# Two more node tiles by count matrices in layer 3, layer 4's input loads on ScalarE's queue, and the early products dealt over 48 steps

## The chip, the cores and the metric

The kernel runs on one NeuronCore of a Trainium2 chip. What counts is the device time of one execution in microseconds. The median of three runs of the kernel before is 2790.45 us (2781.69 to 2791.27). TensorE (PE) multiplies, VectorE (DVE) and ScalarE (ACT) work elementwise, GpSimd (POOL) issues the indirect gathers, and SyncE (SP) issues DMAs. Each engine works off its own instructions in order, waits included.

## The reference, cut to what matters

The input is a graph with 6250 nodes and 100000 edges, sorted by destination, and `x` with 256 features a node. Four graph layers follow each other, and the result is added to `x`:

```
h = relu(layernorm(x))
h = sage_mean(h)   # h@W_self + (segment_sum(h[src], dst) / max(deg,1))@W_neigh + b   256 -> 512
h = sage_pool(h)   # hmax = segment_max(relu(h@W_pool + b)[src], dst); h@W_self + hmax@W_neigh + b
h = sage_gcn(h)    # (segment_sum(h[src], dst) + h) / (deg + 1) @ W_neigh + b
h = sage_mean(h)   # like the first, 512 -> 512
out = x + h@W_fc + b_fc    # 256 wide
```

All is f32. The products with weights are pulled ahead of the sums where that is possible, so that each layer mainly sums or maximizes rows of a table over the edges of a node.

## The kernel before, in words

The nodes are `NT` = 49 tiles of 128 (the last has 106 rows), the edges `T` = 782 tiles of 128. There are two ways to sum the neighbours of a node tile:

- **By count matrices.** For a node tile `d` and a source tile `s` a 128 x 128 matrix holds how many edges lead from each node of `s` to each of `d`. These are made once and stored in fp8 in `tab_a`. `dense` (L555 to 579) then takes one product of a count matrix and the rows of `s` after the other (L566 where the rows are f32, L574 where they are split into bf16 or f32r parts, L572 for a tile's own rows) and adds them up in a PSUM bank `pd`.
- **By gathers.** `sums` (L468) takes the edge tiles from node tile `h` on: GpSimd gathers 128 source rows into a slot of `ring` (L492), VectorE makes a one-hot of the destinations (L488), TensorE multiplies both (L513 for bf16 parts, three matmuls each, L510 for f32), and VectorE adds the groups' banks `pg` into the node tile's `acc` (L542, L544). Between two gathers `sums` calls `hub.advance`, which issues a share of the products of the first kind, and moves on generators that finish a node tile.

`HUB` = (H1, H3, H4) = (8, 18, 22) says how many of the first node tiles, which have the most edges, are summed by count matrices in layers 1, 3 and 4.

*Layer 2* (max-pooling, about 732 to 1915 us) runs over 782 steps `at`. In each, GpSimd gathers 128 rows (L1688) and VectorE carries running maxima through them (L1669, called from L1694 to L1705). Beside these steps count matrices are made (up to step `EARLY_AT` = 310), finished node tiles go through `done2` (products `pm_prf`, L1552 to 1558), and their rows for layer 3 go to table `tab_r`. The rows of tiles 8 to 39 (`EARLY`) also go straight into layer 3's sums: `early_products` (L1626) takes them in eight batches and, for each of the first H3 node tiles, issues a load `ae<-tab_a` on SP (L1637), a cast to f32r on ScalarE (L1624), the products (L574, L572) and an add into `acc3[d]` on VectorE (L1306; a tile's first by a copy on ScalarE, L1309). L1732 to 1734 deal this work out: at each step they issue what is left, divided by the number of steps, 32 or less.

*Layer 3* (about 1945 to 2363 us) takes the other source tiles (0 to 7 and 40 to 48) by count matrices for the first 18 node tiles, 43 matmuls a tile (L1878), and all edges of the other node tiles by 314 gathers of `tab_r` (384 KB each). `done3` (L1834) stores halves of the result into `tab_s` (L1865) and a part of the output, `xq` (L1866). Some tiles' halves (`z4_kept`, 12 tiles) stay in SBUF for layer 4.

*Layer 4* (from about 2363 us) loads the others (`z4_late`, 37 tiles, `resident`, L1817, 256 KB a tile), and sums 22 node tiles by count matrices. These stream in chunks: `ac<-tab_a` loads on ScalarE's queue (L1785), casts `af<-ac` on ScalarE two chunks ahead (L1794), 1078 matmuls (L566). The other edges go by 266 gathers of `tab_s`. A node tile ends in `load4` and `finish4`: `load4` loads the rows of `x` and of `xq` into `xr4` and `q4`, of which there are 7 buffers each (L1893, L1895); VectorE adds both (L1909) and twice a scaled half of the sum (L1911), and SP stores the tile from the same buffer `xr4` (L1914). So a load into `xr4` waits until the store of the tile seven before has landed.

A scheduler puts the instructions of each engine into their order when the kernel is built: as a rule it moves a load up to where its buffer comes free, and other work by its own estimates, so the order is not that of the source.

## Time and profile before

| | us |
|---|---|
| median of three runs | 2790.45 |
| lowest, highest | 2781.69, 2791.27 |
| the profiled execution | 2779.08 |
| its span in the trace | 2777.2 |

| stage (us from the start of the span) | length | PE busy | DVE busy | POOL busy |
|---|---|---|---|---|
| layer 1, 0 to 712 | 712 | 621 | 552 | 506 |
| layer 2, 732 to 1915 | 1183 | 914 | 1015 | 801 |
| layer 3, 1945 to 2363 | 418 | 393 | 290 | 313 |
| layer 4, 2363 to 2777 | 414 | 344 | 222 | 254 |

The times of the stages are from one profiled execution, whose granted TensorE clock was 0.915 on the mean. A row of a view of groups or of waits has the engine, the line and the tiles; in a timeline row the start, the duration, the engine, the line, the operation, the output and inputs, the count, and in brackets the idle time before it and what ended it. A matmul's duration in such a row is its whole passage; what it costs the engine is the distance of the starts.

### The profile page before, as it was taken

How to read it: one execution, taken by the hardware profiler on the slowest of the kernel's cores; microseconds unless marked ns; L12 is line 12 of the kernel's file. 1: busy time of each engine (PE TensorE's matmuls, PEld its weight loads, DVE VectorE, ACT ScalarE, POOL GpSimd, SP SyncE). 2: the span in 40 equal slices, each digit the busy share in tenths (PEclk: the TensorE clock that was granted, in tenths of full speed). 3: DMA queues.
4: the chain of work that ended last, by engine and by line, in shares of the span. 5: the costliest groups of instructions: out<-in, count | busy, mean ns of one | idle time of the engine just before them, and what ended most of it. 6: DMA issues, size and time to landing. Idle time of an engine off the chain costs nothing.

```text
span 2777.2 us, 37443 instructions
## 1 busy us (share of the span) xinstructions
PE 2299.6 (83%) x10201; PEld 1418.2 (51%) x10256; DVE 2092.7 (75%) x5568; ACT 1287.6 (46%) x2837; POOL 1877.5 (68%) x2193
## 2 busy tenths in 40 slices
PE   4698999999695566567899999994899999688887
PEld 2356667667443222234555666462444444466776
DVE  8888767766699898796788998786567777355656
ACT  4567767764388888785332333231101010243443
POOL 5477777777567676676656766764777777556664
PEclk8799999999897678688899999997999999799998
DMA  8567777777799999899999999997999999989886
GB/s 269 157 185 204 206 210 215 223 227 219 248 354 323 305 350 325 290 353 346 319 289 317 352 344 307 322 318 234 386 380 392 388 390 358 333 283 294 286 279 201
DMA packets 364121, 818.00 MB, mean 295 GB/s; under 512 B 56271, under 2 KB 151607, under 8 KB 363869
## 3 DMA queue, kind: packets, MB, share of 16 engines
q0 software_dynamic: 145168, 511.30, 56.6%
q1 hardware_dynamic: 157696, 227.59, 22.8%
q10 hardware_dynamic: 61036, 76.62, 8.0%
q8 instruction: 84, 1.38, 0.2%
q14 instruction: 137, 1.11, 0.1%
HBM read 610.63 MB, written 205.46 MB: 294 GB/s over the span
## 4 chain that ended last, share of the span: by engine, by line
PE 42%; DMA 32%; DVE 11%; issue 5%; ACT 4%; POOL 3%; ACTq 0%; SPq 0%; DVEq 0%; POOLq 0%
PE pd L574 13%; PE pg L513 9%; DMA X<-rows,srcIf 8%; DMA ring<-tab_r,srcE 5%; DMA ring<-tab_h,srcT 4%; DVE run L1669 3%; DMA out<-xr 3%; PE pm_hp L1175 3%; PE pm_prf L1558 2%; DMA xr<-in_x 2%; PE pm_w L277 2%; PE pm_hp L1169 2%; DMA rows<-X 2%; DMA zt<-tab_s 2%; PE pb L349 2%
## 5 line engine op out<-in xcount | busy, mean ns | idle before, releaser
L1688 POOL DMA_INDIRECT X<-rows,srcIf x782 | 742.8, 950 | 360.4 <-issue 147.0
L1669 DVE SCALAR_TENSOR_TENSOR run<-run,samef,X 128x512 f32<-128x512 f32 x758 | 571.8, 754 | 49.8 <-DMA X<-rows,srcIf 44.6
L492 POOL DMA_INDIRECT ring<-tab_h,srcT x474 | 455.6, 961 | 149.9 <-issue 52.5
L513 PE MATMUL pg<-ring,hot 128*128 128x256 bf16 (+2 forms) x2344 | 493.1, 317 | 59.2 <-DMA ring<-tab_h,srcT 29.3
L492 POOL DMA_INDIRECT ring<-tab_r,srcE x314 | 314.9, 1003 | 116.2 <-issue 46.3
L544 DVE SCALAR_TENSOR_TENSOR acc<-pg,M,acc 128x256 f32<-128x256 f32 (+2 forms) x629 | 322.5, 539 | 84.4 <-PE pg L513 70.9
L1794 ACT CAST af<-ac 128x768 fp32r<-128x768 fp8e4 (+3 forms) x212 | 171.0, 808 | 435.5 <-DMA ac<-tab_a 175.1
L492 POOL DMA_INDIRECT ring<-tab_s,srcE x266 | 254.2, 955 | 150.9 <-PE pg L510 80.7
L513 PEld LDWEIGHTS <-hot 128*128 128x128 bf16 x2364 | 220.8, 98 | 261.2 <-issue 127.3
L566 PE MATMUL pd<-zt,af 128*128 128x512 f32 x1078 | 309.9, 416 | 30.4 <-ACT af L1794 16.8
L1669 DVE SCALAR_TENSOR_TENSOR X<-X,samef,run 128x512 f32<-128x512 f32 x379 | 281.7, 743 | 40.6 <-DMA X<-rows,srcIf 22.5
L574 PE MATMUL pd<-kept_rows,aw 128*128 128x512 f32 x828 | 259.6, 438 | 11.1 <-ACT aw L1624 5.6
L566 PEld LDWEIGHTS pd<-zt,af 128*128 128x128 f32 x1078 | 215.2, 201 | 86.8 <-ACT af L1794 23.9
L488 DVE TENSOR_SCALAR hot<-iota_bf,keyE 128x128 bf16<-128x128 bf16 (+1 forms) x580 | 147.2, 279 | 97.7 <-PE pg L513 52.0
L1558 PE MATMUL pm_prf<-unf,hTf 128*128 128x512 f32 x384 | 204.3, 659 | 1.9 <-ACT hTf L1548 1.3
L574 PEld LDWEIGHTS pd<-kept_rows,aw 128*128 128x128 f32 x828 | 157.7, 193 | 73.3 <-issue 29.8
L341 ACT ACTIVATE hs<-ht,onef 128x128 bf16<-128x128 bf16 x396 | 153.6, 393 | 87.7 <-PE pb L349 86.6
L574 PE MATMUL pd<-Z,A 128*128 128x256 bf16 (+1 forms) x1176 | 184.1, 273 | 0.9 <-ACT A L354 0.8
L1624 ACT CAST aw<-ae 128x512 fp32r<-128x512 fp8e4 x144 | 89.3, 621 | 161.3 <-PE pd L574 142.8
L375 ACT ACTIVATE ht<-iota_bf,skR 128x128 bf16<-128x128 bf16 x448 | 158.2, 402 | 10.4 <-DMA col<-in_L_gnn_b 7.2
L340 ACT ACTIVATE ht<-iota_bf,sk 128x128 bf16<-128x128 bf16 x396 | 153.2, 398 | 8.3
L488 DVE TENSOR_SCALAR hot<-iota_bf,keyT 128x128 bf16<-128x128 bf16 x474 | 125.4, 274 | 39.5 <-PE pg L513 38.4
(391 smaller groups left out, 4087.9 us busy)
## 6 DMA issues: line engine op xcount, KB each, us to landing
rows<-X SPq DMA_DIRECT2D x385, 256.0 KB
tab_r<-r ACTq DMA_DIRECT2D x48, 384.0 KB
rows<-hpf SPq DMA_DIRECT2D x49, 256.0 KB
th<-tab_t ACTq DMA_DIRECT2D x49, 256.0 KB
X<-rows,srcIf POOLq DMA_INDIRECT x782
tab_a<-A ACTq DMA_DIRECT2D x14, 784.0 KB
ac<-tab_a ACTq DMA_DIRECT2D x110, 96.0 KB
tab_t<-th SPq DMA_DIRECT2D x37, 256.0 KB
```

Source lines behind the costliest of these rows:

```text
L341: nc.scalar.activation(hots[0], t, AF.Relu, bias=one, scale=-1.0)
L375: nc.scalar.activation(held["ht"][:, i, :], iota_b, AF.Abs, bias=sk[:, r : r + 1])
L488: nc.vector.tensor_scalar(hot[j], iota_b, keyT[:, j - jb : j - jb + 1], None, op0=ALU.is_equal)
L492: nc.gpsimd.indirect_dma_start(out=ring[:, j % deep, :].bitcast(F32) if wide else ring[:, j % deep, :], out_offset=None, in_=table, in_off ...
L513: mm = nc.tensor.matmul(pg[:, : F + c], hot[j], X[:, part * F : (part + 1) * F + c], start=(k == 0 and part == 2), stop=(k == n - 1 and pa ...
L544: nc.vector.scalar_tensor_tensor(acc[d], half, m, acc[d], op0=ALU.mult, op1=ALU.add)
L566: nc.tensor.matmul(hold[0], a, z, start=(s == ss[0]), stop=(s == ss[-1]))
L574: nc.tensor.matmul(hold[0][:, : F + c], a, z[:, part * F : (part + 1) * F + c], start=(first and s != own), stop=(s == ss[-1] and part == ...
L1558: nc.tensor.matmul(pm, hT[:, c, :], un[:, c, :], start=False, stop=(c == KH - 1))
L1669: nc.vector.scalar_tensor_tensor(put, held, st, row, op0=ALU.mult, op1=ALU.max)
L1688: nc.gpsimd.indirect_dma_start(out=X[:, k, :], out_offset=None, in_=tab_p, in_offset=bass.IndirectOffsetOnAxis(ap=srcI[:, t : t + 1], axis=0),
L1794: nc.scalar.copy(wide[i][:, :n, :], got[i][:, :n, :])
```

## The change

Three things change. H3 goes from 18 to 20: node tiles 18 and 19 are summed in layer 3 by count matrices. (These exist already, since layer 4 uses 22 tiles.) The early products are dealt over 48 steps where it was 32. In layer 4 the loads of `x` and `xq` are issued on ScalarE's queue, with ten buffers each, and the tiles that stay in SBUF are now 10 (33 to 42), with 39 loaded back.

```diff
@@ -28,7 +28,7 @@
 BLOCKS = (52, 100, 220, 180, 130, 100)
 Z_SIGMA = 5.0
 WIN, WIN2 = 8, 4
-HUB = (8, 18, 22)
+HUB = (8, 20, 22)
 EARLY = (8, 40)
 MADE_AT = 64
 FIRST_AT = 112
@@ -1731,7 +1731,7 @@
                         copies.pop(0)()
                     if at > EARLY_AT + 10:
                         early.advance(early.done + math.ceil(
-                            early.left() / max(1, min(32, T - 24 - at))))
+                            early.left() / max(1, min(48, T - 24 - at))))
                     if b == 0 and s0 == 0 and k == 0:
                         for _ in finding:
                             pass
@@ -1824,8 +1824,8 @@
         psm = on.enter_context(tc.tile_pool(name="psm3", bufs=2, space=PSUM))
         zk = on.enter_context(tc.tile_pool(name="fz4", bufs=1, side="right"))
         Z4 = {}
-        z4_kept = ((31, 37), (37, 43))
-        z4_late = ((0, 7), (7, 14), (14, 20), (20, 26), (26, 31), (43, NT))
+        z4_kept = ((33, 38), (38, 43))
+        z4_late = ((0, 7), (7, 14), (14, 20), (20, 27), (27, 33), (43, NT))
         for s0, s1 in z4_kept:
             zt = zk.tile([P, s1 - s0, 2 * FO], F32R, name=f"zt{s0}", bufs=1)
             Z4.update({s: zt[:, s - s0, :] for s in range(s0, s1)})
@@ -1889,10 +1889,10 @@
 
             def load4(d):
                 n = P if d < NFULL else NREM
-                xr = wk.tile([P, FI], F32, name="xr4", bufs=7)
-                nc.sync.dma_start(xr[:n, :], x[d * P : d * P + n, :])
-                q = wk.tile([P, FO], F32, name="q4", bufs=7)
-                nc.sync.dma_start(q[:n, :], xq[d * P : d * P + n, :])
+                xr = wk.tile([P, FI], F32, name="xr4", bufs=10)
+                nc.scalar.dma_start(xr[:n, :], x[d * P : d * P + n, :])
+                q = wk.tile([P, FO], F32, name="q4", bufs=10)
+                nc.scalar.dma_start(q[:n, :], xq[d * P : d * P + n, :])
                 loaded4[d] = n, xr, q
 
             def done4(d, acc):
```

On the engines' orders this gives: L574 has 3316 matmuls, before 3102, L572 40, before 36, and L513 2292, before 2364; 290 gathers of `tab_r`, before 314; 140 adds at L1306, before 126; 160 loads and casts `ae`, `aw`, before 144. The matmuls at L566 and L510 and the gathers of `tab_s` stay as many.

SyncE in the middle of layer 4, before. `xr4_...` are allocations of the residual buffers, numbers grow in program order; `in_x` is the input, `xq_70` the part of the output from layer 3:

```order
L1914 DMA out_0<-xr4_25672 128x256
L1893 DMA xr4_26104<-in_x 128x256
L1914 DMA out_0<-xr4_25557 128x256
L1893 DMA xr4_26171<-in_x 128x256
L1895 DMA q4_26653<-xq_70 128x256
L1895 DMA q4_26666<-xq_70 128x256
L1914 DMA out_0<-xr4_25720 128x256
L1893 DMA xr4_26267<-in_x 128x256
```

The same engine after, at the same stores of layer 4:

```order
L1914 DMA out_0<-xr4_25846 128x256
L1914 DMA out_0<-xr4_25716 128x256
L1914 DMA out_0<-xr4_25884 128x256
L1914 DMA out_0<-xr4_26016 128x256
L1914 DMA out_0<-xr4_25993 128x256
```

Only the stores are left. Before, the load into `xr4_26104` waited for the store from `xr4_25672` ahead of it, since it takes its buffer, and the store from `xr4_25557` stood behind that load.

ScalarE after, at the same place. `af` is a cast chunk of count matrices, `ac` a loaded one:

```order
L1794 CAST af_25877<-ac_25751 128x768
L1785 DMA ac_25955<-tab_a_69 128x384
L1794 CAST af_25912<-ac_25770 128x896
L1893 DMA xr4_26504<-in_x 128x256
L1785 DMA ac_25974<-tab_a_69 128x384
L1794 CAST af_25931<-ac_25792 128x768
L1785 DMA ac_25988<-tab_a_69 128x320
L1893 DMA xr4_26554<-in_x 128x256
L1794 CAST af_25953<-ac_25811 128x768
L1895 DMA q4_27226<-xq_70 128x256
```

The load into `xr4_26504` waits for the landing of the store from `xr4_25846`, that into `xr4_26554` for the one from `xr4_25716`; the casts behind them wait with them. Before, this queue had only casts and `ac` loads here.

VectorE in layer 4, before: from the last use of a buffer (`xr4_26005`) to the add on the tile that is loaded into it next (`xr4_26488`). `acc` are sums of node tiles, `hot` one-hots:

```order
L1911 SCALAR_TENSOR_TENSOR xr4_26005<-pd_25846,rmeanf_128,xr4_26005 128x256 x2
L544 SCALAR_TENSOR_TENSOR acc_25832<-pg_25998,M_125,acc_25832 128x256
L488 TENSOR_SCALAR hot_26095<-iota_bf_109,keyE_10816 128x128
L544 SCALAR_TENSOR_TENSOR acc_25832<-pg_25998,M_125,acc_25832 128x256
L544 SCALAR_TENSOR_TENSOR acc_25995<-pg_25998,M_125,acc_25995 128x256
L488 TENSOR_SCALAR hot_26115<-iota_bf_109,keyE_10816 128x128
L544 SCALAR_TENSOR_TENSOR acc_25995<-pg_25998,M_125,acc_25995 128x256
L488 TENSOR_SCALAR hot_26127<-iota_bf_109,keyE_10816 128x128
L1909 TENSOR_TENSOR xr4_26386<-xr4_26386,q4_26388 128x256
L488 TENSOR_SCALAR hot_26139<-iota_bf_109,keyE_10816 128x128
L1909 TENSOR_TENSOR xr4_26488<-xr4_26488,q4_26490 128x256
```

After: from the row behind the last use of `xr4_25683` to the add on the tile that takes its buffer, `xr4_26341`:

```order
L544 SCALAR_TENSOR_TENSOR acc_25443<-pg_25663,M_125,acc_25443 128x256
L488 TENSOR_SCALAR hot_25763<-iota_bf_109,keyE_10816 128x128
L544 SCALAR_TENSOR_TENSOR acc_25443<-pg_25663,M_125,acc_25443 128x256
L544 SCALAR_TENSOR_TENSOR acc_25558<-pg_25663,M_125,acc_25558 128x256
L1911 SCALAR_TENSOR_TENSOR xr4_25552<-acc_25443,rmeanf_128,xr4_25552 128x256
L544 SCALAR_TENSOR_TENSOR acc_25558<-pg_25663,M_125,acc_25558 128x256
L542 TENSOR_SCALAR acc_25722<-pg_25663,M_125 128x256
L488 TENSOR_SCALAR hot_25783<-iota_bf_109,keyE_10816 128x128
L544 SCALAR_TENSOR_TENSOR acc_25722<-pg_25663,M_125,acc_25722 128x256
L488 TENSOR_SCALAR hot_25796<-iota_bf_109,keyE_10816 128x128
L488 TENSOR_SCALAR hot_25804<-iota_bf_109,keyE_10816 128x128
L1909 TENSOR_TENSOR xr4_26341<-xr4_26341,q4_26343 128x256
```

Between last use and add stand nine instructions before, and eleven after.

VectorE in layer 2, in the first round of the early products, before. `X` and `run` are the running maxima, `acc_0` to `acc_2` the sums `acc3` of node tiles 0 to 2:

```order
L1306 TENSOR_TENSOR acc_0_10818<-acc_0_10818,pd 128x512
L1669 SCALAR_TENSOR_TENSOR X_17206<-X_17206,samef,run 128x512
L1669 SCALAR_TENSOR_TENSOR run<-run,samef,X_17206 128x512
L1306 TENSOR_TENSOR acc_1_10819<-acc_1_10819,pd 128x512
L1669 SCALAR_TENSOR_TENSOR run<-run,samef,X_17226 128x512
L1669 SCALAR_TENSOR_TENSOR X_17226<-X_17226,samef,run 128x512
L1306 TENSOR_TENSOR acc_2_10820<-acc_2_10820,pd 128x512
```

After, at the same adds:

```order
L1306 TENSOR_TENSOR acc_0_10818<-acc_0_10818,pd 128x512
L1669 SCALAR_TENSOR_TENSOR run<-run,samef,X_17285 128x512
L1669 SCALAR_TENSOR_TENSOR X_17285<-X_17285,samef,run 128x512
L1669 SCALAR_TENSOR_TENSOR run<-run,samef,X_17285 128x512
L1669 SCALAR_TENSOR_TENSOR run<-run,samef,X_17308 128x512
L1669 SCALAR_TENSOR_TENSOR X_17308<-X_17308,samef,run 128x512
L1669 SCALAR_TENSOR_TENSOR run<-run,samef,X_17308 128x512
L1306 TENSOR_TENSOR acc_1_10819<-acc_1_10819,pd 128x512
L1669 SCALAR_TENSOR_TENSOR run<-run,samef,X_17325 128x512
L1306 TENSOR_TENSOR acc_2_10820<-acc_2_10820,pd 128x512
```

The adds now stand further apart, with more rows of running maxima between the first two.

## The prediction

> **What bounds the kernel now.** I read first the table of busy time by stretches, cut at the stages that the change touches: the part of layer 2 that carries layer 3's early products, layer 3, the start of layer 4, and layer 4 itself.
>
> ```profile
> core 0: us, PE busy (x) PEld busy (x) DVE busy (x) ACT busy (x) POOL busy (x), PEclk, DMA share, GB/s
> 1290.00:1895.00 605.00, 558.08 (x1939) 353.12 (x1959) 498.09 (x744) 201.97 (x356) 399.96 (x422) 0.96 0.95 320
> 1945.00:2363.00 418.00, 392.64 (x1709) 188.96 (x1742) 290.11 (x679) 41.30 (x84) 312.50 (x312) 0.99 1.01 381
> 2363.00:2440.00 77.00, 52.45 (x168) 38.26 (x168) 24.80 (x78) 19.50 (x24) 42.85 (x45) 0.80 0.95 339
> 2440.00:2767.00 327.00, 291.69 (x1177) 229.34 (x1177) 193.89 (x601) 129.66 (x153) 211.31 (x221) 0.94 0.86 274
> ```
>
> TensorE is the fullest engine in each stage: 558 of 605 us, 393 of 418, 292 of 327. But busy time on PE is stretched by waiting, so I asked next, for each stage, which work the chain that ends last is made of. In this order: 1500 to 1700 us (layer 2), 1945 to 2360 (layer 3), 2428 to 2777 (layer 4).
>
> ```profile
> by line: PE pd L574 45.7%; PE pm_prf L1558 19.0%; PE pm_prf L1552 9.5%; PE pm_prf L1555 9.4%; DMA X<-rows,srcIf 5.5%; PE pt_hTf L1545 2.4%; DMA ae<-tab_a 1.7%; PE pm_prf L1578 1.5%; PE pm_prf L1572 1.3%; PE pm_prf L1588 1.2%; POOL X L1688 1
> ```
> ```profile
> by line: DMA ring<-tab_r,srcE 33.9%; PE pg L513 30.0%; PE pd L574 25.0%; POOL ring L492 4.3%; issue 4.2%; DMA xq<-q 1.3%; DVE acc L544 0.5%; PE pd L572 0.4%; DVE q L1837 0.2%; DVE q L1838 0.2%; PE pm_own L1857 0.2%; DVE hot L488 0.1%; POOLq
> ```
> ```profile
> by line: DMA out<-xr 25.2%; DMA xr<-in_x 17.9%; PE pd L566 13.4%; DVE acc L544 9.8%; DMA q<-xq 5.4%; issue 4.6%; DVE xr L1911 4.4%; DVE hot L488 4.1%; DMA ac<-tab_a 4.1%; PE pg L510 3.5%; DVE xr L1909 2.6%; ACT af L1794 1.3%; DVE acc L542 0
> ```
>
> In layer 2 the chain is nearly all TensorE. In layer 3 two thirds are TensorE, a third the landing of gathers. In layer 4 TensorE has 17%, while the store of a finished tile, the load of the next input tile and the load of `q` together hold 25.2 + 17.9 + 5.4 = 48.5%. Two neighbouring pieces of that chain, and the two waits that belong to them, tell what this is:
>
> ```profile
> 2558.51 4.49 DMA out<-xr
> 2563.06 4.41 DMA xr<-in_x
> ```
> ```profile
> SPq L1893 <- DMA out<-xr: 111.1, 38, 4.6
> ```
> ```profile
> L1909 DVE TENSOR_TENSOR xr<-xr,q 128x256 f32<-128x256 f32 (+1 forms) x49 | 20.8, 427 | 136.1 <-DMA xr<-in_x 91.2 <-DMA ac<-tab_a 25.0 <-DMA q<-xq 11.5
> ```
>
> SP's queue stands 111 us in front of input loads until an output store has landed, because the buffer that is loaded is the one that is being stored. VectorE's in-order queue then stands 136 us in front of the residual add for that load. Meanwhile finished sums aren't evacuated, PSUM banks and ring slots stay taken, and TensorE and GpSimd wait for those.
>
> **The change, layer 2.** Two more node tiles by count matrices, each over 32 early source tiles and its own rows in two parts, mean 2 x 2 x 33 = 132 more matmuls. They come in eight batches a tile: 16 more loads and casts, and 14 more adds (a tile's first batch is copied, not added).
>
> ```profile
> 1708.99 19.11 PE pd L574 x82
> ```
> ```profile
> L1306 DVE TENSOR_TENSOR acc<-acc,pd 128x512 f32<-128x512 f32 x126 | 86.0, 682 | 17.2 <-PE pd L574 16.3
> L1624 ACT CAST aw<-ae 128x512 fp32r<-128x512 fp8e4 x144 | 89.3, 621 | 161.3 <-PE pd L574 142.8 <-DMA ae<-tab_a 12.3 <-issue 4.3
> ```
> ```profile
> ae<-tab_a SPq DMA_DIRECT2D x144, 64.0 KB
> ```
> ```profile
> 1495.00:1720.00 225.00, 222.38 (x803) 143.58 (x812) 203.69 (x295) 80.80 (x140) 152.53 (x161) 1.00 0.98 338
> ```
>
> PE: 132 x 19.11/82 = 132 x 0.233 = 30.8 us. VectorE: 14 x 0.682 = 9.5 us. ScalarE: 16 x 0.621 = 9.9 us, hidden, as it is busy 202 of 605 us. DMA: 16 x 64 KB = 1 MB, at 320 GB/s 3.3 us. The stretch has 605 - 558 = 47 us of idle PE and 107 of idle VectorE. So the cost lies between nothing (all 31 us fall into the 47) and 31 + 9.5 = 40 us (PE is the chain, and its adds too). Dealing the work over 48 steps and not 32 fills gaps earlier, and by the order fewer running-max rows are left behind the last adds. But the last row, of the middle of the stretch, has PE busy 222 of 225 us: there are no gaps there to fill. I take 10 us, a third of the PE work: nearer to nothing, because the idle 47 us are more than the 31 needed; not nothing, because only 2.6 of them lie in this middle. If that cover is gone, it costs 31 to 40 us (case C).
>
> **Layer 3.** The two tiles' remaining products come in, 43 matmuls each, with four casts on a ScalarE that is busy 41 of 418 us. 24 gathers with three matmuls each go: 86 - 72 = 14 more matmuls.
>
> ```profile
> 2342.20 0.81 PE L513 MATMUL pg<-ring,hot 128*128 128x512 bf16 x3
> 2342.85 0.81 PE L574 MATMUL pd<-zt,ac 128*128 128x512 bf16 x3
> 2343.50 0.81 PE L513 MATMUL pg<-ring,hot 128*128 128x512 bf16 x3
> ```
> ```profile
> ring<-tab_r,srcE POOLq DMA_INDIRECT x314
> ```
> ```profile
> 1945.77 0.95 POOL ring L492
> 1947.02 0.95 POOL ring L492
> ```
>
> Starts of three are 0.65 us apart, 0.217 for one, with nothing between: 14 x 0.217 = +3 us. A gather takes GpSimd 1.25 us from start to start, so 24 x 1.25 = 30 us leave it, and 24 x 384 KB = 9.4 MB leave the DMA, 25 us at 381 GB/s. Where TensorE sets the pace this frees nothing but its scattered waits: I take 0 for all this, between -6 (a quarter of the 25 us that PE is idle in the stage) and +3. If the gathers set the pace, it is -25 (case D).
>
> Here I weighed a rule. The three rows show matmuls back to back, a weight load beneath each, and that is a full TensorE. The Trainium skill ("Trainium Kernel Development and Optimization", section Performance Expectations) calls the busy share of matmuls a poor measure, and asks for the share of weight loads instead. By that rule 188.96 of 418 us (45%), beside a DMA share of 1.01, is a TensorE kept waiting for data, and dropping gathers pays; the sum would then be 25 us lower. That is case D below.
>
> **Start of layer 4.** Two kept tiles fewer stay in SBUF, so 39 and not 37 tiles of `tab_s` (256 KB each) are loaded back: 0.5 MB, at 339 GB/s 1.5 us on the path, since the products wait for these loads. The four matmuls that the kept tiles no longer give as cover are 4 x 0.23 = 0.9 us, which the same loads hide.
>
> **Layer 4.** All outputs stay on SP; the input and `q` loads go to ScalarE's queue, and both have ten buffers, not seven. Before, the loop of a buffer is: store 4.49 us, load 4.41 us, then the add, together 8.9 us. Against it stands the VectorE work that lies in its order between the last use of the freed buffer and the add on the newly loaded one, at these prices:
>
> ```profile
> 2567.50 0.43 DVE xr L1909
> 2567.93 0.39 DVE acc L544
> 2568.32 0.19 DVE hot L488
> ```
>
> Counted over all the reloads that the order has: 3.9 us before (42 reloads), 4.65 us after (39), so the three extra buffers buy little cover. The larger part is the queue. Before, the second store of a pair stands on SP behind a load that waits for the first store's landing, so two tiles pay one loop after the other; after, stores never stand behind loads. VectorE's wait was 136.1/24.5 = 5.5 us a pair of tiles. After, I expect one loop less its cover, 8.9 - 4.65 = 4.25 us: 24.5 x 1.3 = 31 us less, and three reloads fewer at 136.1/49 = 2.8 us each, 8 more. Together 39 us less waiting.
>
> What is late next? The gathers of layer 4, 221 spans on POOL in this stretch, and its matmuls:
>
> ```profile
> 2560.66 0.95 POOL L492 DMA_INDIRECT ring<-tab_s,srcE  x1 [0.31 <-PE pg L510]
> 2561.91 0.95 POOL L492 DMA_INDIRECT ring<-tab_s,srcE  x1 [0.30 <-PE pd L566]
> ```
> ```profile
> 2712.72 1.07 PE L566 MATMUL pd<-zt,af 128*128 128x512 f32 x4
> 2713.62 0.39 PE L510 MATMUL pg<-ring,hot 128*128 128x512 f32 x1
> 2713.85 1.08 PE L566 MATMUL pd<-zt,af 128*128 128x512 f32 x4
> ```
>
> GpSimd needs 221 x 1.25 = 276 us, 51 less than 327. PE needs 1.13 us for five, so 1177 x 0.226 = 266 us, 61 less. Neither caps the 39. The new danger is ScalarE, whose queue now holds 39 waits for stores, with the casts for TensorE queued behind them:
>
> ```profile
> 2564.01 0.94 ACT L1794 CAST af<-ac 128x896 fp32r<-128x896 fp8e4 x1 [0.45 <-ACT af L1794]
> 2564.98 0.33 ACTq L1785 DMA_DIRECT2D ac<-tab_a  x1
> 2565.40 0.94 ACT L1794 CAST af<-ac 128x896 fp32r<-128x896 fp8e4 x1 [0.45 <-ACT af L1794]
> ```
> ```profile
> ACT af L1794 <- PE pd L566: 129.4, 78, 11.3
> ```
>
> A cast and its load take 1.4 us, and before ScalarE waited 129 us for TensorE to free a cast buffer, so it has slack, and the casts run two chunks ahead (12 matmuls, 2.7 us) before TensorE feels a wait. A wait of a whole landing, 4.5 us, is more than that; in the order most of these loads stand some six chunks behind the tile they wait for, and so mostly find it stored. I take off a quarter of the 39: -30 us. Ends: -50 (the GpSimd cap) and +10 (VectorE gains nothing, and 24 loads, one a pair, each hold the casts so long that TensorE loses 0.4 us).
>
> **Sum.** +10 + 0 + 1.5 - 30 = -18.5 us. The profiled execution took 2779.1 us, which gives 2760.6; it lies 11.4 us below the median of the runs, 2790.45, so on that footing 2772 us.
>
> **The rivals.** *B, nothing is gained in layer 4.* The loads still wait for the same landings, only on another queue; VectorE's add comes as late as before, or ScalarE's casts do. For it: 4.65 us of cover against a loop of 8.9. Against it: the SP wait of 111 us is a wait for a landing in front of other stores, which the change takes away. The Trainium skill speaks for B ("DMA: Bandwidth & Descriptors", section Issuing engines are not separate DMA queues): issuing from several engines only saves the issuing time of a sequencer, usually little. The row for that issue time:
>
> ```profile
> 2563.06 0.33 SPq L1893 DMA_DIRECT2D xr<-in_x  x1
> ```
>
> Here 98 loads x 0.33 = 32 us of issuing move away from SP, which isn't short of issue time, so by that rule the move is worth nothing. The time of B: 2790.45 + 10 + 1.5 = 2802.
>
> *C, slower: TensorE in layer 2 has no room.* Place: 1290 to 1895 us. The 31 us of matmuls and 9.5 us of adds go on the path in full, because the idle 47 us lie in stalls that remain. With half of my gain in layer 4 (-15) it turns the sum positive once layer 2 costs more than 13.5 us; at the full 40 us it is +40 + 1.5 - 15 = +26.5, so 2817. For it: the chain of 1500 to 1700 us, nearly all PE. Against it: 47 us is more than the 40 that are added, and 48 steps have more of these gaps within them than 32.
>
> *D, layer 3 is bound by its gathers.* Then 25 us more go: 2772 - 25 = 2747. For it: a DMA share of 1.01 and 33.9% of the chain on gathers. Against it: the gapless rows above.
>
> **How the numbers follow.** Chances: forecast 0.45, B 0.25, C 0.15, D 0.15. Half a per cent, about what a measurement of this kernel can tell from no change, is 14 us: faster is below 2776.5, slower above 2804.4. The forecast's own range, 2757 to 2794, lies two thirds below 2776.5: 0.29 faster, 0.15 the same, 0.01 slower. D is faster (0.15). B at 2802 splits: 0.14 the same, 0.11 slower. C gives 0.02 the same and 0.13 slower. Together 0.44, 0.31, 0.25. The range reaches from a little under D to a little under C: 2742 to 2813.
>
> **What would show it.** Right: in the changed profile SP's wait for stores is gone; VectorE's wait before L1909 falls from 136 us to about 100; the layer-4 stretch shrinks by about 30 us; layer 2 ends about 10 us later; layer 3 takes the same 418 us within 6. B: L1909's wait stays near 136, or TensorE's waits for casts at L1794 grow by as much. C: layer 2 ends 25 us or more later. D: layer 3 is 20 us or more shorter. I am wrong altogether if the change in time comes from none of these stages, or if the clock granted to TensorE differs from the 0.96 to 0.99 of these stretches.

## The result, and the profile after

The changed kernel takes 2743.38 us (median of four runs, 2741.85 to 2745.26). The kernel before took 2788.17 us (median of four, 2781.69 to 2791.27). The ratio is 0.9843, with a 95% interval of 0.9822 to 0.9863: 44.8 us less, where the prediction had 18.5 less. The two profiled executions differ by 36.9 us (2779.08 and 2742.18), and the stages below are theirs. Several experiments fell on stretches, on more than one chip, in which the kernel before took 3130 to 3200 us and not some 2780; they are called the slowed stretch here, and each of their ratios is against runs of the kernel before on the same chip in the same group.

Where the time came from is read from three rows of GpSimd's gathers, as layer 2 begins with the first gather of `X`, layer 3 with that of `tab_r`, and layer 4 with that of `tab_s`. The two numbers before the semicolon are the starts of the first and the last gather. Before:

```profile
L1688 POOL DMA_INDIRECT X<-rows,srcIf x782: 940/946/1462, 732.7 to 1914.0; - x196
L492 POOL DMA_INDIRECT ring<-tab_r,srcE x314: 942/946/1723, 1941.9 to 2354.6; - x157
L492 POOL DMA_INDIRECT ring<-tab_s,srcE x266: 940/946/1340, 2367.8 to 2759.6; - x133
```

After (the span is 2740.4 us, before 2777.2):

```profile
L1688 POOL DMA_INDIRECT X<-rows,srcIf x782: 940/946/1400, 731.4 to 1923.2; - x196
L492 POOL DMA_INDIRECT ring<-tab_r,srcE x290: 940/946/1799, 1951.4 to 2343.4; - x145
L492 POOL DMA_INDIRECT ring<-tab_s,srcE x266: 940/946/1252, 2357.8 to 2722.7; - x133
```

| stage, first gather to first gather | before | after | difference | predicted |
|---|---|---|---|---|
| layer 2 | 1209.2 | 1220.0 | +10.8 | +10 |
| layer 3 | 425.9 | 406.4 | -19.5 | 0 |
| layer 4, up to the first sum taken from a bank `pd` (L1911) | 61.8 | 67.9 | +6.1 | +1.5 |
| layer 4, the rest | 347.6 | 314.7 | -32.9 | -30 |

Layer 1 has another 1.3 us less. Layer 3 is the term that was missed: it comes near case D, which had 25 us, and 20 or more as its sign. The sum of the other three came near what was measured. But the cut within layer 4 doesn't divide the same work: of the 49 adds on input rows (L1909) one lies ahead of it before, and ten lie ahead of it after. Uncut, layer 4 took 409.4 us before and 382.6 after, 26.8 less, where the prediction had 28.5 less.

Layer 3's chain of waits (after, 1945 to 2340 us) shows what went: the landing of gathers held 33.9% of it before.

```profile
by line: PE pd L574 45.7%; PE pg L513 43.3%; DMA ring<-tab_r,srcE 4.7%; POOL ring L492 2.4%; issue 1.1%; PE pd L572 0.8%; DMA tab_r<-r 0.6%; ACT r L1502 0.4%; DVE q L1838 0.2%; DVE acc L544 0.2%; PE pm_own L1857 0.2%; ACT r L1598 0.1%; ACT 
```

Now it is nearly all TensorE. The same is seen in 50 us from the middle of layer 3, first before, then after (columns: the stretch and its length, then busy time and count for PE, PEld, DVE, ACT and POOL, the granted clock, the DMA share and GB/s):

```profile
2191.90:2241.90 50.00, 47.85 (x212) 22.73 (x215) 34.67 (x84) 4.98 (x11) 38.39 (x39) 1.00 1.02 394
```
```profile
2201.40:2251.40 50.00, 50.00 (x230) 24.60 (x228) 36.37 (x86) 6.14 (x12) 38.41 (x37) 1.00 1.02 386
```

230 matmuls at 0.217 us are 49.9 us: after the change TensorE never waits there. Before it did 212, and GpSimd started 39 gathers, one in 1.28 us, close to the 1.25 us that most of them take (239 of the 313 distances are at most 1.26 us). The place is no exception: the eight stretches of 50 us from 1950 to 2350 us have 202 to 221 matmuls before, and the five from 2060 to 2310 us have 229 or 230 after.

GpSimd, in turn, had no pause in layer 3 before. Of the 313 gaps between its gathers 305 are the 0.30 us of these rows from the middle (at most 0.35), and the other eight are 3.3 us longer in all:

```profile
2154.00 0.94 POOL L492 DMA_INDIRECT ring<-tab_r,srcE  x1 [0.30 <-issue]
2155.25 0.95 POOL L492 DMA_INDIRECT ring<-tab_r,srcE  x1 [0.30 <-issue]
2156.50 0.95 POOL L492 DMA_INDIRECT ring<-tab_r,srcE  x1 [0.30 <-issue]
```

57 of the 314 took over 1.00 us, 17.5 us more than at 0.95; what held those no row names. 313 x 1.25 + 17.5 + 3.3 = 412 us is all the time from the first gather to the last, 412.7.

In layer 4 VectorE tells the story. These are its waits before the add (L1909) from the cut to the end, before and after:

```profile
DVE xr L1909 <- DMA xr<-in_x: 91.2, 27, 6.0
DVE xr L1909 <- DMA ac<-tab_a: 25.0, 8, 5.1
DVE xr L1909 <- DMA q<-xq: 11.5, 6, 3.9
DVE xr L1909 <- issue: 8.3, 2, 5.8
```
```profile
DVE xr L1909 <- DMA xr<-in_x: 94.2, 30, 6.2
DVE xr L1909 <- issue: 3.2, 1, 3.2
DVE xr L1909 <- DMA out<-xr: 1.7, 1, 1.7
```

Together 136.0 us before and 99.1 us after, 36.9 less; this part became 32.9 us shorter. A good part of that has only moved: the nine adds that now lie ahead of the cut waited there, and over the whole of layer 4 the wait fell from 136.1 to 124.4 us:

```profile
L1909 DVE TENSOR_TENSOR xr<-xr,q 128x256 f32<-128x256 f32 (+1 forms) x49 | 20.8, 426 | 124.4 <-DMA xr<-in_x 94.2 <-DMA q<-xq 25.3 <-issue 3.2
```

VectorE's busy time behind the cut hardly changed, as its column shows in the rows of the same stretches (202.30 before, 199.50 after):

```profile
2429.60:2777.20 347.60, 302.09 (x1223) 237.47 (x1221) 202.30 (x623) 133.78 (x158) 215.56 (x226) 0.94 0.84 269
```
```profile
2425.70:2740.40 314.70, 286.52 (x1222) 228.16 (x1220) 199.50 (x613) 133.86 (x158) 214.51 (x224) 0.98 0.88 287
```

Busy time and this one wait make 202.3 + 136.0 = 338 of 348 us before, and 199.5 + 99.1 = 299 of 315 us after. Behind the cut VectorE's queue is what layer 4 runs by, before and after.

At the start of layer 4 the loads on ScalarE's queue hold casts back. Two waits ahead of the cut, after the change, and the longest of ScalarE's idle times there (before, TensorE's own wait for casts was 5.7 us; its wait for loads of `tab_s` went the other way, from 13.6 to 5.7):

```profile
ACT af L1794 <- DMA q<-xq: 16.7, 2, 15.4
PE pd L566 <- ACT af L1794: 14.8, 4, 5.6
```
```profile
2400.97 0.94 ACT L1794 CAST af<-ac 128x896 fp32r<-128x896 fp8e4 x1 [15.38 <-DMA q<-xq]
```

Seven of these 15 us pass before the load of a chunk of count matrices goes out, at 2392.58 us, and the others while six of the first loads into the ten empty buffers do. The cast stands behind both.

### The profile page after: what moved, and what is told of

Same layout as the page of the kernel before. It is cut to its first block, busy times and chain, and to the rows that moved or that the text cites. A ratio compares the mean times of both kernels' runs of the same rounds, so it can differ in the third digit from the quotient of the medians.

```text
span 2740.4 us, 37738 instructions
## 1 busy us (share of the span) xinstructions
PE 2314.7 (84%) x10402; PEld 1439.0 (53%) x10402; DVE 2088.1 (76%) x5540; ACT 1299.7 (47%) x2859; POOL 1857.0 (68%) x2169
## 4 chain that ended last, share of the span: by engine, by line
PE 48%; DMA 24%; DVE 13%; ACT 5%; issue 4%; POOL 2%; ACTq 0%; DVEq 0%; SPq 0%; POOLq 0%
PE pd L574 17%; PE pg L513 11%; DMA X<-rows,srcIf 7%; DMA xr<-in_x 4%; DVE run L1669 4%; DMA ring<-tab_h,srcT 4%; PE pm_hp L1175 3%; DMA rows<-X 3%; PE pm_prf L1558 3%; PE pm_hp L1169 2%; PE pd L566 2%; PE pb L349 2%; DVE acc L544 2%; DVE X L1669 2%; PE pm_prf L1552 2%
## 5 line engine op out<-in xcount | busy, mean ns | idle before, releaser
L513 PE MATMUL pg<-ring,hot 128*128 128x259 bf16 (+1 forms) x2292 | 475.1, 316 | 41.9 <-DMA ring<-tab_h,srcT 29.1
L544 DVE SCALAR_TENSOR_TENSOR acc<-pg,M,acc 128x256 f32<-128x256 f32 (+2 forms) x617 | 314.3, 536 | 80.9 <-PE pg L513 69.1
L492 POOL DMA_INDIRECT ring<-tab_r,srcE x290 | 293.3, 1011 | 116.2 <-issue 48.5
L566 PE MATMUL pd<-zt,af 128*128 128x512 f32 x1078 | 302.9, 407 | 38.1 <-ACT af L1794 31.6
L513 PEld LDWEIGHTS <-hot 128*128 128x128 bf16 x2292 | 214.3, 98 | 226.4 <-issue 103.6
L574 PE MATMUL pd<-kept_rows,aw 128*128 128x512 f32 x920 | 292.2, 440 | 11.2 <-ACT aw L1624 6.3
L566 PEld LDWEIGHTS pd<-zt,af 128*128 128x128 f32 x1078 | 208.7, 196 | 95.8 <-ACT af L1794 44.6
L574 PEld LDWEIGHTS pd<-kept_rows,aw 128*128 128x128 f32 x920 | 174.7, 192 | 83.9 <-issue 35.3
L1624 ACT CAST aw<-ae 128x512 fp32r<-128x512 fp8e4 x160 | 99.4, 622 | 181.3 <-PE pd L574 163.9
L574 PE MATMUL pd<-Z,A 128*128 128x256 bf16 (+1 forms) x1176 | 184.8, 274 | 0.7 <-ACT A L354 0.6
L393 PE MATMUL pb<-hm,hs 128*128 128x196 bf16 x448 | 82.3, 281 | 89.8 <-ACT A L398 65.4
```

Source lines behind the costliest of these rows:

```text
L492: nc.gpsimd.indirect_dma_start(out=ring[:, j % deep, :].bitcast(F32) if wide else ring[:, j % deep, :], out_offset=None, in_=table, in_off ...
L513: mm = nc.tensor.matmul(pg[:, : F + c], hot[j], X[:, part * F : (part + 1) * F + c], start=(k == 0 and part == 2), stop=(k == n - 1 and pa ...
L544: nc.vector.scalar_tensor_tensor(acc[d], half, m, acc[d], op0=ALU.mult, op1=ALU.add)
L566: nc.tensor.matmul(hold[0], a, z, start=(s == ss[0]), stop=(s == ss[-1]))
L574: nc.tensor.matmul(hold[0][:, : F + c], a, z[:, part * F : (part + 1) * F + c], start=(first and s != own), stop=(s == ss[-1] and part == ...
```

## The experiments

The theory after the result: layer 3 was paced by GpSimd, and 24 gathers fewer let TensorE's pace come through; layer 4 gains from the queue of the loads. The rivals: layer 3 was paced by TensorE, or by the bytes of the gathers; layer 4 gains from the buffers and not the queue, or from the new division of the kept tiles.

### Leaving out 24 gathers, and nothing else

```
-                gather(j)
+                if F != FH or wide or j - j0 < 12 or (j - j0) % 12 or (j - j0) // 12 > 24:
+                    gather(j)
```

> The kernel before, in which layer 3 leaves out every twelfth of its gathers, 24 in all; their matmuls, one-hots and adds stay and read what the ring slot held. TensorE's work is that of before. Theory (layer 3 was paced by GpSimd, gather after gather, 314 x 1.25 = 392 us of its 426 us): where gathers run as in the first comparison layer 3 falls to 400 to 410 us; where all is slower, as in the first two groups of experiments (471 us), to 434 to 444 us. Rival (paced by TensorE, and its 14 more matmuls and fewer stores or own-row adds made the changed kernel's layer 3 shorter in some other way): it stays within 6 us of 426, or of 471.

Measured: 2758.51 us, one run, beside 2774.14 us for one run of the kernel before. Layer 3, from the rows below, took 2346.5 - 1939.8 = 406.7 us.

```profile
L492 POOL DMA_INDIRECT ring<-tab_r,srcE x290: 940/946/1899, 1939.8 to 2331.1; - x145
L492 POOL DMA_INDIRECT ring<-tab_s,srcE x266: 940/946/1250, 2346.5 to 2737.1; - x133
```
```profile
1939.80:2346.50 406.70, 385.50 (x1709) 189.13 (x1742) 293.23 (x693) 42.25 (x86) 293.24 (x290) 0.98 0.99 371
```

The matmuls (1742 weight loads, as before) are all there, and the stage is as short as in the changed kernel, within the 400 to 410 us foretold. So TensorE's work did not set layer 3's pace; the gathers did. The bytes of the 24 went with them, so this run alone doesn't part their number from their bytes; for the number speaks that GpSimd had no pause between them (above): had the bytes landed too late, a gather would have had to wait for its slot of the ring.

The edit leaves layer 4 as it was, so this run also tells how well a stage repeats: with the same cut it took 62.9 and 347.3 us, beside 61.8 and 347.6, and the wait before the add was 136.7 us in all, beside 136.1.

### Only H3 = 20

```
-HUB = (8, 18, 22)
+HUB = (8, 20, 22)
```

and the new `z4_kept` and `z4_late`, without which layer 3 doesn't fit into SBUF.

> Only H3 goes to 20 (with the division of the kept tiles that it needs for space); 32 steps, and layer 4's loads on SP with 7 buffers, are as before. Stages are cut at the first gather of tab_r and of tab_s. Theory (layer 3 was paced by its gathers, and 24 fewer bring it down to TensorE's pace): layer 2 about 10 us longer, layer 3 406 us where it was 426, layer 4 within 8 us of the 409 of before; in all 0.996 to 1.000 of before. Rival (the prediction's: layer 3 is paced by TensorE, and what it lost came from the other edits): layer 3 stays at 426 within 6 us, and the time is 1.002 to 1.006.

Measured in the slowed stretch: 3124.44 us beside 3150.87, ratio 0.9912 (0.9881 to 0.9944), better than either number. Layer 3 took 435.8 us. A kernel of the same group with layer 3 as before, the loads alone (below), had 471.1 us there. First that one, then this:

```profile
L492 POOL DMA_INDIRECT ring<-tab_r,srcE x314: 940/946/1723, 2262.0 to 2718.8; - x157
L492 POOL DMA_INDIRECT ring<-tab_s,srcE x266: 940/946/1597, 2733.1 to 3139.0; - x133
```
```profile
L492 POOL DMA_INDIRECT ring<-tab_r,srcE x290: 940/946/1726, 2272.8 to 2694.7; - x145
L492 POOL DMA_INDIRECT ring<-tab_s,srcE x266: 940/946/1419, 2708.6 to 3102.0; - x133
```

A gather came every (2718.8 - 2262.0)/313 = 1.46 us there; 24 of them are 35 us, and the stage lost 35.3. That agrees with the theory, but shows it less well than the run above, since GpSimd does pause there: 37 gaps in the first of these kernels are over 0.35 us, 46.2 us above 0.30 in all, like the second one here.

```profile
2460.55 0.95 POOL L492 DMA_INDIRECT ring<-tab_r,srcE  x1 [0.30 <-issue]
2463.04 0.94 POOL L492 DMA_INDIRECT ring<-tab_r,srcE  x1 [1.54 <-PE pd L574]
```

Layer 4, which has only the new division of the kept tiles here, took 414.0 us, beside 415.5 in the kernel of the same group that comes next and has layer 4 as before. So the division gave next to nothing there.

### A third of the bytes of layer 3's gathers taken away

```
-                out=ring[:, j % deep, :].bitcast(F32) if wide else ring[:, j % deep, :],
-                out_offset=None, in_=table,
+                out=(ring[:, j % deep, :].bitcast(F32) if wide else
+                     ring[:, j % deep, : 2 * F] if F == FH else ring[:, j % deep, :]),
+                out_offset=None, in_=(table.rearrange("r f -> (r f)").rearrange("(r f) -> r f", f=2 * F)
+                     if F == FH and not wide else table),
```

The ring's last third is set to zero once.

> The kernel before, with each gather of layer 3 fetching 2 KB a row and not 3 KB, from wrong places of the table (the third part of the rows is zeros); all its matmuls, one-hots and adds stay. Theory (layer 3 was paced by the bytes of its gathers): layer 3 falls from 426 us to 385 to 405, with TensorE at 228 matmuls in 50 us where it had 205 to 215. Rival (paced by TensorE): it stays at 420 to 426 us. A third way, paced by GpSimd's 1.3 us for each gather and not by bytes: also 415 to 426 us, with gathers still 1.3 us apart.

> The kernel before with 2 KB and not 3 KB a gathered row in layer 3 (its third part zeros, the rows from wrong places), a second time. Paced by the bytes of the gathers: layer 3 385 to 405 us where before has 426. Paced by TensorE or by GpSimd's time for each gather: 415 to 426 us. On the slower chip it would again be the same as before there (467 us beside 471).

> The kernel before with 2 KB instead of 3 KB a gathered row in layer 3, again, since both of the first fell on slowed chips. Now that layer 3 has been seen to fall to 407 us when 24 gathers are left out: if the pace of the gathers is that of their bytes, layer 3 falls to 385 to 405 us; if it is GpSimd's 1.25 us for each gather whatever its size, it stays at 415 to 426 us.

All three fell on the slowed stretch: 3151.47, 3157.47 and 3135.45 us, one run each, beside 3150.87, 3147.94 and 3147.91. Layer 3 took 466.9, 467.7 and 468.2 us; with all bytes it was 471.1, 470.1 and 471.5 in the same groups. The row of layer 3 of the first, and below it that of the kernel with all bytes:

```profile
2267.30:2734.20 466.90, 411.38 (x1743) 191.09 (x1743) 294.24 (x696) 41.74 (x86) 319.01 (x314) 0.96 0.81 255
```
```profile
2262.00:2733.10 471.10, 405.44 (x1743) 188.26 (x1742) 291.34 (x693) 41.97 (x86) 316.34 (x314) 0.98 0.95 340
```

The DMA share fell from 0.95 to 0.81 and the stage by 4 us. There the bytes don't pace layer 3; but GpSimd pauses in these three as well (31 to 42 longer gaps, 41 to 48 us above 0.30). Whether the bytes matter outside the slowed stretch, where the share is 1.02, no run shows.

### The loads alone

```
-                xr = wk.tile([P, FI], F32, name="xr4", bufs=7)
-                nc.sync.dma_start(xr[:n, :], x[d * P : d * P + n, :])
-                q = wk.tile([P, FO], F32, name="q4", bufs=7)
-                nc.sync.dma_start(q[:n, :], xq[d * P : d * P + n, :])
+                xr = wk.tile([P, FI], F32, name="xr4", bufs=10)
+                nc.scalar.dma_start(xr[:n, :], x[d * P : d * P + n, :])
+                q = wk.tile([P, FO], F32, name="q4", bufs=10)
+                nc.scalar.dma_start(q[:n, :], xq[d * P : d * P + n, :])
```

> Only layer 4's loads go to ScalarE's queue with 10 buffers; H3 is 18, 32 steps. Theory (the loads by themselves give the gain of layer 4): layers 2 and 3 as before, layer 4 from the first gather of tab_s to the end 380 to 388 us where it was 409, the time 0.990 to 0.993. Rival (layer 4 gains from what layer 3 leaves behind, or from the new division of the kept tiles): layer 4 stays over 400 us, the time 0.997 to 1.001.

> Layer 4's loads on ScalarE's queue with 10 buffers, the rest as before; a second time, since on the slower chip it brought nothing (1.0009). Theory (it brings layer 4's gain where the chip is not slowed): layer 4 380 to 390 us where before has 409, the time 0.988 to 0.994. Rival (it brings nothing anywhere, and layer 4 gained from what came ahead of it): layer 4 over 400 us, the time 0.997 to 1.003.

> The two loads of layer 4 on ScalarE's queue with 10 buffers, all else as before; a third time, since the first two fell on chips on which every stage took longer. Theory (the loads give layer 4's gain by themselves): layer 4 from 409 to 380 to 390 us, layers 2 and 3 as before, the time 0.988 to 0.994. Rival (layer 4 gained from the new division of the kept tiles, or from what layer 3 leaves behind): layer 4 over 400 us, 0.997 to 1.003.

> The two loads of layer 4 on ScalarE's queue with 10 buffers, all else as before, sent by itself: the groups of several kernels ran at some 3150 us for the kernel before, the single ones at 2774 to 2791. Theory (the loads give layer 4's gain): layer 4 from 409 to 380 to 390 us, the time 0.988 to 0.994. Rival (it comes from the division of the kept tiles, or from layer 3's end): layer 4 over 400 us, the time 0.997 to 1.003.

The first three, in the slowed stretch, gave 1.0009 (0.9978 to 1.0040), 1.0004 (0.9977 to 1.0031) and 1.0015 (0.9989 to 1.0040): nothing. The fourth, outside it, gave 0.9913 (0.9889 to 0.9938): 2756.69 us beside 2782.14, with layer 4 at 390.8 us, just over the 380 to 390 foretold.

```profile
L492 POOL DMA_INDIRECT ring<-tab_r,srcE x314: 942/946/1722, 1937.3 to 2352.1; - x157
L492 POOL DMA_INDIRECT ring<-tab_s,srcE x266: 940/946/1260, 2365.0 to 2739.4; - x133
```
```profile
2365.00:2433.90 68.90, 43.37 (x125) 30.11 (x126) 20.47 (x67) 15.01 (x19) 39.23 (x42) 0.72 1.01 358
2433.90:2755.80 321.90, 291.03 (x1220) 231.83 (x1219) 200.70 (x614) 132.90 (x158) 214.87 (x225) 0.97 0.88 283
```

Layer 3 stays at 427.7 us. The loads, by their queue and their three more buffers, give 18.6 of layer 4's 26.8 us without the other edits, and with it the longer stretch up to the cut, 68.9 us, with ten adds ahead of it here too.

### The loads back on SP, ten buffers kept

```
-                nc.scalar.dma_start(xr[:n, :], x[d * P : d * P + n, :])
+                nc.sync.dma_start(xr[:n, :], x[d * P : d * P + n, :])
-                nc.scalar.dma_start(q[:n, :], xq[d * P : d * P + n, :])
+                nc.sync.dma_start(q[:n, :], xq[d * P : d * P + n, :])
```

> The changed kernel with the loads back on SP, still with 10 buffers. If the queue gives the gain of layer 4 (theory): layer 4 is 400 to 412 us where the changed kernel has 383, and the time 0.991 to 0.995 of before. If the three more buffers give it (rival): layer 4 stays within 8 us of 383, and the time is 0.983 to 0.987.

> The changed kernel with the loads back on SP's queue, with 10 buffers; a second time, on the chip of the two above. If the queue gives layer 4's gain: slower than the changed kernel by 0.6 to 1.0 per cent, layer 4 over 400 us. If the buffers give it: the same as the changed kernel within 0.3 per cent. If ScalarE's queue costs and the buffers gain: faster than the changed kernel by 0.3 per cent or more.

> The changed kernel with its loads back on SP, 10 buffers kept; again, as the first two fell on slowed chips. If ScalarE's queue gives layer 4's gain: layer 4 400 to 412 us where the changed kernel has 383, the time 0.989 to 0.995. If the three more buffers give it: 375 to 390 us, the time 0.981 to 0.987.

> The changed kernel with its loads back on SP, 10 buffers kept, sent by itself, after the loads alone gave 0.9913. If ScalarE's queue gives that gain: layer 4 400 to 412 us where the changed kernel has 383, the time 0.990 to 0.995. If the three more buffers give it: 375 to 390 us, the time 0.981 to 0.987.

> The changed kernel with its loads back on SP, 10 buffers kept, once more by itself. Where the kernel before takes some 2780 us: if ScalarE's queue gives the gain of layer 4, layer 4 is 400 to 412 us where the changed kernel has 383; if the three more buffers give it, 375 to 390 us. Where it takes some 3150 us: 412 to 416 us again, and nothing is told apart.

> The changed kernel with its loads back on SP, 10 buffers kept, by itself again. Where the kernel before takes some 2780 us: if ScalarE's queue gives the gain of layer 4, layer 4 is 400 to 412 us where the changed kernel has 383; if the three more buffers give it, 375 to 390 us. Where it takes some 3150 us: 412 to 416 us again, and nothing is told apart.

In the slowed stretch the ratios were 0.9877 (0.9843 to 0.9911), 0.9913 (0.9880 to 0.9946), 0.9936 (0.9913 to 0.9959) and 0.9887 (0.9817 to 0.9957), and one run of 3112.92 beside 3147.83 us, with layer 4 at 412 to 416 us. Outside it one run took 2745.39 us beside 2790.07, a ratio of 0.984, which the earlier expectations had given for the buffers. Its stages say otherwise:

```profile
L1688 POOL DMA_INDIRECT X<-rows,srcIf x782: 943/949/1449, 730.6 to 1912.2; - x196
L492 POOL DMA_INDIRECT ring<-tab_r,srcE x290: 943/949/1794, 1939.0 to 2330.4; - x145
L492 POOL DMA_INDIRECT ring<-tab_s,srcE x266: 943/949/1229, 2344.8 to 2723.9; - x133
```
```profile
2344.80:2405.00 60.20, 43.06 (x125) 30.47 (x126) 17.39 (x58) 13.97 (x18) 39.68 (x42) 0.78 1.02 386
2405.00:2743.50 338.50, 292.10 (x1221) 227.49 (x1219) 202.80 (x622) 133.99 (x158) 215.37 (x225) 0.98 0.86 275
```
```profile
DVE xr L1909 <- DMA xr<-in_x: 72.9, 23, 6.0
DVE xr L1909 <- DMA ac<-tab_a: 32.8, 10, 4.8
DVE xr L1909 <- DMA q<-xq: 14.2, 8, 5.0
DVE xr L1909 <- DMA out<-xr: 3.5, 1, 3.5
```

This splits layer 4's gain. It took 398.7 us here, just under the 400 to 412 us foretold for the queue: of the 26.8 us, 16.1 are the queue's, and 10.7 come with the ten buffers and the new division of the kept tiles. (With the 18.6 us of the loads alone, and if the parts add up, 2.5 of these are the buffers'.)

Behind the cut the queue seems to give more, 338.5 - 314.7 = 23.8 us, and to cost 67.9 - 60.2 = 7.7 us ahead of it, but that is again the cut, since one add lies ahead of it here. These are the first and the last input load, here and in the changed kernel:

```profile
L1893 SPq DMA_DIRECT2D xr<-in_x x49: 263/333/554, 2389.6 to 2698.4; - x49
```
```profile
L1893 ACTq DMA_DIRECT2D xr<-in_x x49: 266/340/553, 2369.2 to 2695.1; - x49
```

On SP the first of them goes out 44.8 us into layer 4, behind six loads of `tab_s`; on ScalarE's queue it goes out after 11.4 us. The first ten adds then wait 25.3 us and not 6.7, but early, where VectorE has little else to do (it is busy 20.8 of the 67.9 us). The other 39, whose loads reuse a buffer, wait 99.1 us and not 116.8. The eleventh add comes 76.4 us into the stage, here 77.5, and from there to the end it takes 306.2 us, here 321.2. So the queue gives its 15 us from there on, with 17.7 us less of that wait. What the held casts cost doesn't show in the time of the eleventh add, though TensorE has done 156 matmuls a microsecond ahead of it, here 193. The clock has no part in this, as it is 0.98 behind the cut with both queues. SP's own wait in front of the input loads is still long here, where it was 111.1 us before; in the changed kernel SP has only stores.

```profile
SPq L1893 <- DMA out<-xr: 95.9, 31, 5.5
```

That its time is yet no worse than the changed kernel's is due to layer 2, which took 1939.0 - 730.6 = 1208.4 us here and 1220.0 there, though up to layer 4 both have the same instructions in the same order on every engine. So layer 2's time differs by 12 us between these two executions, for a reason that isn't in its instructions and that these runs don't show.

### The changed kernel once more

> The changed kernel once more, on the chip of this group of runs, so that its stages can be set against those of its variants there. Where the chip is like the one of the first comparison: 0.982 to 0.987 of before, layer 3 406 us, layer 4 383 us. Where gathers and loads take longer throughout, as they did in the first group of experiments (before took 3151 us there): the same ratio within 0.006 if the change acts in the same way; above 0.990 if the loads on ScalarE cost there what layer 3 gains.

It fell on the slowed stretch: 3123.75 us beside 3147.94, ratio 0.9918 (0.9887 to 0.9950), the lower of the gains foretold. Layer 3 was 436.0 us (470 to 471 with 314 gathers), so it gains there too. Layer 4 was 421.8 us, longer than the 412 to 416 with the loads on SP: the queue gives nothing there.

### Stores from a tile of their own

```
+                o = wk.tile([P, FO], F32, name="o4", bufs=4)
                 for c in range(0, acc.shape[1], FO):
-                    nc.vector.scalar_tensor_tensor(xr[:n, :], acc[:n, c : c + FO],
+                    nc.vector.scalar_tensor_tensor((o if c + FO == acc.shape[1] else xr)[:n, :],
+                                                   acc[:n, c : c + FO],
...
-                nc.sync.dma_start(out[d * P : d * P + n, :], xr[:n, :])
+                nc.sync.dma_start(out[d * P : d * P + n, :], o[:n, :])
```

> The changed kernel, in which the last scaled sum goes to a tile of its own (four of these), and SP stores from that: a load into the residual buffer then waits for VectorE's last use of it, but not for the store's landing. If the loop of store, load and add still sets layer 4's pace: VectorE's wait before the add falls from 124 us to under 60, layer 4 from 383 to 350 to 370 us, the time 0.970 to 0.980 of before. If something else sets the pace by now (GpSimd's 266 gathers at 1.25 us, 333 us, or TensorE): layer 4 stays within 8 us of 383.

> The changed kernel, in which the last scaled sum goes to a tile of its own (four of these) and SP stores from that, so that a load waits for VectorE's last use of its buffer but not for the store's landing; by itself this time. Where the kernel before takes some 2780 us: if the loop of store, load and add still sets layer 4's pace, VectorE's wait before the add falls from 124 us to under 60, layer 4 from 383 to 350 to 370 us, the time to 0.970 to 0.980 of before. If something else sets the pace by now (GpSimd's 266 gathers at 1.25 us are 333 us; TensorE), layer 4 stays within 8 us of 383. Where the kernel before takes some 3150 us: 0.988 to 0.996 and layer 4 at 412 to 420 us, as the first time.

Both fell on the slowed stretch: 0.9922 (0.9892 to 0.9952) and 0.9933 (0.9902 to 0.9964), beside 0.9918 for the changed kernel. Layer 4 was 416.3 and 423.5 us, the second over the 412 to 420 foretold for it. VectorE's wait before the add in the first of them, and below it that of the changed kernel there:

```profile
L1909 DVE TENSOR_TENSOR xr<-xr,q 128x256 f32<-128x256 f32 (+1 forms) x49 | 20.6, 424 | 45.0 <-DMA xr<-in_x 22.6 <-issue 13.3 <-DMA q<-xq 8.8
```
```profile
L1909 DVE TENSOR_TENSOR xr<-xr,q 128x256 f32<-128x256 f32 (+1 forms) x49 | 20.8, 426 | 60.2 <-issue 29.8 <-DMA xr<-in_x 17.3 <-DMA q<-xq 9.8
```

There the wait is only half as long to begin with, 60.2 us beside 124.4, and in the second run of this kernel it was 64.6 us. Whether the edit would gain outside the slowed stretch is open.

## Why the prediction was wrong, point by point

**What failed: layer 3.** The step was this: "Where TensorE sets the pace this frees nothing but its scattered waits: I take 0 for all this, between -6 (a quarter of the 25 us that PE is idle in the stage) and +3." Measured: -19.5 us. TensorE didn't set the pace; GpSimd did, which issued one gather after the other without a pause. I had the two floors in hand and didn't hold them against each other: 314 gathers x 1.25 us = 392 us for GpSimd, 1742 matmuls x 0.217 us = 378 us for TensorE, and the stage took 426. In layer 4 I did make that comparison. I also read the stage's chain as two thirds TensorE; its row gives 56%, and 38% to the landing and issuing of gathers. The three rows without a gap that decided it for me, at 2342 us, lie at the stage's end; in 50 us of its middle TensorE did 212 matmuls where 230 fit. GpSimd's 75% busy share hid that it was full, since the 0.30 us ahead of each gather don't count as busy. Afterwards the floors are 290 x 1.25 = 362 and 1756 x 0.217 = 381: the bound has changed over to TensorE, which is why 24 gathers gave 19.5 us and not the 24 x 1.25 = 30 that they take of GpSimd, nor the 25 us of case D, which went by bytes. The run without 24 gathers shows this part: 406.7 us with TensorE's work unchanged.

The Trainium skill's rule ("Trainium Kernel Development and Optimization", section Performance Expectations), against which I decided, pointed the right way: the weight loads' share was 45%. What a full TensorE has here can now be read: 24.60 of 50 us, 49%, where it never waits. By that measure it was at some nine tenths before.

**Layer 2, right in size:** +10.8 us for +10, within 0 to 40. But the same instructions took 11.6 us less in another execution, so the cost of the 132 matmuls is somewhere from 0 to 11 us and the agreement is partly luck. Case C, 25 us or more, is out.

**Start of layer 4:** +6.1 us for +1.5, up to the cut. The two more loaded tiles cost nothing to be seen (60.2 us with the loads on SP, 61.8 before); the stretch is 7.7 us longer with ScalarE's queue than with SP's, but by the eleventh add VectorE is no later. That the held casts make the cut later is likely and not shown: the adds ahead of it wait as well.

**Layer 4, right in its direction, near in its sum, not in its parts:** -26.8 us with its start, for -28.5. I had 31 us for the queue and 8 for the buffers, less a quarter for ScalarE; measured are 16.1 for the queue and 10.7 for buffers and division together. SP's wait in front of loads is gone, as foretold. But VectorE's wait did not fall from 136 us to about 100: it fell to 124.4, by 11.7 where I expected 39, and what helped as well, that the first ten adds now wait early in the stage, I hadn't thought of. That the sum came out is partly luck. Case B, nothing gained in layer 4, is out outside the slowed stretch: the queue saved 16.1 us, with the first loads no longer behind those of `tab_s`, nor stores behind loads that wait; how much each of the two gives, no run parts. In the slowed stretch B is what came: the loads alone gave nothing, three times.

The rule that spoke for B is that of the Trainium skill ("DMA: Bandwidth & Descriptors", section Issuing engines are not separate DMA queues), that another issuing engine saves only the issuing time. It holds in the slowed stretch, and not outside.

**The sum:** the other three terms make +10.8 + 6.1 - 32.9 = -16.0 us, where I had -18.5. Layer 3's 19.5 are the whole difference by the profiles. The medians differ by 8 us more than the profiles, as the profiled execution of before was faster than any of its four runs in that comparison; no stage is known for these 8 us. In the chances, 53% of the forecast's range, and not two thirds, lie below 2776.5 us; the sum doesn't hang on that.

## What to carry to other kernels

For each stage, hold the engines' floors against each other, number of instructions times the distance of their starts, before naming the bound; a busy share leaves out what an engine spends ahead of each instruction. Three rows without a gap tell of the place they are from: count the matmuls in several equal stretches. When a load waits for a buffer's store, look at what stands behind it in the queue of its issuing engine, and try the two on different queues. And before you subtract parts of a stage from each other, see that your cut has the same instructions ahead of it in both kernels.

## What the runs showed of the hardware

A gather of 128 rows took 1.25 us of GpSimd from start to start in most cases, of which 0.95 us count as busy, so that GpSimd was full at a busy share of 75%; in layer 3 before, its mean was 412.7/313 = 1.32 us. A TensorE that never waits showed 229 or 230 matmuls of 128x512 in 50 us, one in 0.217 us, and weight loads for 49% of the time. A DMA that had to wait held up what stood behind it in its engine's queue: SP stood 111.1 us in front of input loads for stores to land, and on SP the first input load of layer 4 went out 44.8 us into it, on ScalarE 11.4.
